# Layer 0's attention with seven PSUM banks in one ring of single places

## The chip, the cores and the metric

One Trainium2 chip; the kernel runs on one of its cores. The metric is the device time of one execution in microseconds (us), the median over several runs. All data are fp32. PSUM, the memory that the tensor engine (PE) writes its products to, has eight banks; one bank takes 128 partitions of 512 fp32 numbers. The other engines are named as in the profile: DVE (vector), ACT (scalar), POOL (GpSimd), SP (sync); PEld are PE's weight loads.

## The reference

Two transformer layers over x of 8 sequences, 512 tokens, width 256; each layer is attention and a mixture of experts, each followed by a residual sum and a layer norm. The change touches layer 0's attention (16 heads of 16 numbers, 8 sequences):

```python
qkv = x @ w_qkv + b_qkv
q, k, v = jnp.split(qkv, 3, axis=-1)          # to heads: [b, h, s, d]
scores = jnp.einsum('bhid,bhjd->bhij', q, k) * attn_scale
scores = jnp.where(j >= i, scores, -jnp.inf)  # i: row, j: column
attn = jax.nn.softmax(scores, axis=-1)
out = jnp.einsum('bhij,bhjd->bhid', attn, v)
out = out @ w_out + b_out                     # then x = layernorm(x + out)
```

A token attends to itself and to later ones. After this come layer 0's experts (seven with weights, two choices per token), layer 1's attention with sigmoid weights, and layer 1's experts.

## The kernel before

**Order.** Everything is issued in an order written out by hand (`tc.manual_schedule()`), so each engine works through its instructions as the Python code issues them. Each tile pool is a ring: the tile that is asked for as the n-th of a pool with `bufs` places lies where tile n - bufs lay, and its first writer waits until the last reader of that one is through.

**PSUM.** `psum(stack, sc, av, mm)` (L86) divides the eight banks into three pools: `sc`, wide places of two banks (`wide()`, L93); `av`, single banks for the sums of attention; `mm`, single banks for everything else (`bank()`, L96). Layer 0 runs with `psum(banks, 3, 1, 1)`: three wide places, one `av`, one `mm`. Layer 1 runs with (2, 2, 2).

**Layer 0's attention** is `waves0` (L1356). A sequence is 16 waves: two groups m of eight heads, two halves t of each with four heads (r = 0 to 3), and four blocks of 128 tokens. A wave g issues, in this order:
- `scores` (L624): four products of 32 rows of PE each, K block jb against the queries up to it, of 512, 384, 256 and 128 columns in the four waves of a group (written S512 to S128 below; L629). They go to two wide places, two heads in each. One exponential on ACT (L638) reads a wide place and writes both halves of a tile e; POOL zeroes the masked corner (`affine_select`, L641).
- on the third of four waves `lowered` (L614): PE turns a tile of row bounds (L619) into a single place, DVE copies it (L621), and a DMA puts it into the rows of q that shift the scores.
- first steps of `beside0` (L1286), the work of other sequences: projections of q and k (`query`, L571, read twice by ACT at L584), values (`value`, L556, read by ACT at L564 and L569), `projected` (L673, read by DVE at L683 and L684), transposes of x (`turned_in`, L539, read by ACT at L548), and small routing steps. Each product takes one single place.
- `greatest` (L595) for the wave six further on: four products again (L600; 128, 256, 384, 512 columns when S has 512, 384, 256, 128; written G below) into two wide places. DVE adds a mask and takes the bound of each row, one instruction a head (L608, `seen`), followed by a read of its accumulator, with which the place is free.
- `gathered` (L648): four products of the last wave's e with the values, into `av` (L653); at the end of a group ACT copies `av` out (L661).
- second steps of `beside0`.

In the places' terms a wave without further steps takes four wide places: S heads 0 and 1, S heads 2 and 3, G heads 0 and 1, G heads 2 and 3. The two places of a quad come from

```python
        def quad(width):
            pair = [wide(), wide()]
            return pair, [pair[r // 2][:, r % 2, :width] for r in range(NHS)]
```

Sequences 0 to 6 run first (112 waves), then layer 0's experts (`experts0`, L1412, PE with wide places, beside them the last steps of sequence 6), then the 16 waves of sequence 7 beside the first steps of layer 1, then layer 1. In sequence 0 and during sequence 3 some steps prepare the router's weights (`router_steps`, L307), one step a wave, through the single place.

Of the kernel before, what the change touches and what calls it, by code (L numbers as in the profile page):

```python
# [12 lines left out]
AF = mybir.ActivationFunctionType  # L13
ALU = mybir.AluOpType
AX = mybir.AxisListType
PSUM = bass.MemoryType.PSUM
# [7 lines left out]
NHS = 4  # L24
# [13 lines left out]
SCALE = 0.25  # L38
# [5 lines left out]
def tile_two_layers(  # L44
# [33 lines left out]
    nc = tc.nc  # L78
# [5 lines left out]
    p = {}  # L84

    def psum(stack, sc, av, mm):  # L86

        for name, bufs in (("sc", sc), ("av", av), ("mm", mm)):
            p[name] = stack.enter_context(
                tc.tile_pool(name=f"p_{name}{sc}", bufs=bufs, space=PSUM)  # L90
            )

    def wide():  # L93
        return p["sc"].tile([P, 2, 512], FP, tag="sc", name="sc")

    def bank():  # L96
        return p["mm"].tile([P, 512], FP, tag="mm", name="mm")
# [289 lines left out]
    moe0 = ExitStack()  # L387
    moew = moe0.enter_context(tc.tile_pool(name="moew", bufs=2, side="right"))
    banks = ExitStack()
    psum(banks, 3, 1, 1)  # L390
    nc.scalar.preload_act_table_set("natural_log_exp_and_others")

    def half(name):

        return att.tile([P, S], FP, tag="half", name=name, bufs=16)

    def pair(name):
        return att.tile([P, 2, S], FP, tag="e", name=name, bufs=5)

    def layer0():  # L400
# [13 lines left out]
        ps = bank()[:, : 2 * KC].rearrange("p (i m) -> p i m", m=KC)  # L414
# [153 lines left out]
                q["lg"] = small.tile([P, NC, 8], FP, tag="lgx0", name="lgx0", bufs=3)  # L568
            nc.scalar.copy(q["lg"][:, c, :], ps[:, D : D + 8])  # L569

        def query(b, m, which, part, place=bank):  # L571
            q = st[b]
            w, bias = (wq_s, bq_t) if which == "q" else (wk_s, bk_t)
            at = part * 256
            ps = place()
            for kc in range(KC):
                nc.tensor.matmul(
                    out=ps[:, :256], lhsT=w[:, kc, m * P : (m + 1) * P],
                    rhs=q["xT"][:, kc, at : at + 256], start=(kc == 0), stop=(kc == KC - 1),
                )  # L580
            for t in range(2):
                if part == 0:
                    q[which, m, t] = half(f"{which}{b}_{m}{t}")
                nc.scalar.activation(  # L584
                    q[which, m, t][:, at : at + 256], ps[:, :256], AF.Identity,
                    bias=bias[:, m, t : t + 1], scale=lanes[:, t : t + 1],
                )


        def quad(width):  # L590

            pair = [wide(), wide()]
            return pair, [pair[r // 2][:, r % 2, :width] for r in range(NHS)]

        def greatest(b, m, t, ib):  # L595
            q = st[b]
            width = S - ib * P
            _, places = quad(width)
            for r in range(NHS):
                nc.tensor.matmul(  # L600
                    out=places[r],
                    lhsT=q["q", m, t][32 * r : 32 * r + 32, ib * P : (ib + 1) * P],
                    rhs=q["k", m, t][32 * r : 32 * r + 32, ib * P :],
                    start=True, stop=True,
                )
            for r in range(NHS):
                seen = wp.tile([P, S], FP, tag="seen", name="seen")
                nc.vector.tensor_tensor_reduce(  # L608
                    out=seen[:, :width], in0=places[r], in1=shade[:, :width], scale=-1.0,
                    scalar=-MASKED, op0=ALU.add, op1=ALU.min,  # L610
                    accum_out=mpads[t][:, r, ib : ib + 1],
                )
# [11 lines left out]
        def scores(b, m, t, jb):  # L624
            q = st[b]
            width = (jb + 1) * P
            tiles, places = quad(width)
            for r in range(NHS):
                nc.tensor.matmul(  # L629
                    out=places[r],  # L630
                    lhsT=q["k", m, t][32 * r : 32 * r + 32, jb * P : (jb + 1) * P],
                    rhs=q["q", m, t][32 * r : 32 * r + 32, :width],
                    start=True, stop=True,
                )
            es = []
            for s in tiles:
                e = pair("e")
                nc.scalar.activation(e[:, :, :width], s[:, :, :width], AF.Exp, scale=SCALE)  # L638

                own = e[:, :, jb * P : width]  # L640
                nc.gpsimd.affine_select(  # L641
                    out=own, in_=own, pattern=[[0, 2], [-1, P]], compare_op=ALU.is_ge, fill=0.0,
                    base=0, channel_multiplier=1,
                )
                es += [e[:, u, :width] for u in range(2)]
            return b, m, t, jb, es
# [709 lines left out]
    def waves0(start, stop):  # L1356
        nonlocal waiting
        t = l0
        for g in range(start, stop):
            b, w = g // 16, g % 16  # L1360
            now = None
            if g >= 0:
                now = t.scores(b, w // 8, w // 4 % 2, NC - 1 - w % 4)
                if w in FILLS:
                    t.fill(b, FILLS.index(w))
                if w == 10 and b + 2 < B:
                    t.load_x(b + 2)
            if g % 4 == 3 and waiting:
                t.gathered(*waiting)
                waiting = None  # L1370
            if (g + 2) % 4 == 0 and 0 <= g + 2 < 16 * B:
                ob, ow = (g + 2) // 16, (g + 2) % 16
                t.lowered(ob, ow // 8, ow // 4 % 2)
            first, second = beside0(b, w if g >= 0 else g)
            if b == 0 and w in (1, 3, 4, 5, 8, 9, 12):
                fn, arg = t.rsteps.pop(0)
                fn(arg)
                if w == 1:
                    t.residual(0)
            if b in (1, 2):  # L1380
                for _ in range(2):
                    if loads:
                        nc.sync.dma_start(**loads.pop(0))
            if 16 * 3 + 10 <= g < 16 * 3 + 10 + len(l1.steps):
                fn, arg = l1.steps[g - 16 * 3 - 10]
                fn(arg)
            run(first)
            ob, ow = (g + AHEAD) // 16, (g + AHEAD) % 16
            if ob < B:
                t.greatest(ob, ow // 8, ow // 4 % 2, (1, 0, 3, 2)[ow % 4])  # L1390
            if waiting:
                t.gathered(*waiting)
            run(second)
            waiting = now
# [229 lines left out]
    l0 = layer0()  # L1624
    loaded = {}
    with tc.manual_schedule():
        for kc in range(KC):
            l0.turned_in(0, kc)
        for which in ("q", "k"):
            for part in range(2):  # L1630
                l0.query(0, 0, which, part, lambda: wide()[:, 0, :])
        waves0(-AHEAD, 16)
        l1 = layer1(Later(), SimpleNamespace(dma_start=lambda **copy: loads.append(copy)))
        waves0(16, 48)
        assert not loads
        for e in range(2):
            loaded[e] = weights0(e)
        waves0(48, 16 * (B - 2))
        h = [half(f"h{f}") for f in range(I0 // P)]
        waves0(16 * (B - 2), 16 * (B - 1) - 3)  # L1640

        xe = att.tile([P, 2, 2, S], FP, tag="o", name="xe", bufs=2)
        xes = {
            e: tokens0(e, xe[:, e].rearrange("p u (c d) -> p (u c) d", d=D)) for e in range(2)
        }
        waves0(16 * (B - 1) - 3, 16 * (B - 1))
        l0.gathered(*waiting)
        waiting = None
        a, z, n = B - 2, B - 3, B - 1
        t = l0  # L1650
        steps = [(t.apart_again, a)]
        steps += [(t.query, n, 1, "q", part) for part in range(2)]
        steps += [(t.inverted, a)]
        steps += [(t.query, n, 1, "k", part) for part in range(2)]
        steps += [(t.kept, z, c) for c in range(NC)]
        steps += [(t.shared, z), (t.pointed, z)]
        steps += [(t.weighed, a, kc) for kc in range(KC)]
        steps += [(t.counted, z), (t.filled,), (t.ranked, z), (t.sent, z)]
        steps += [(t.projected, a, c) for c in range(NC)]
        steps += [(fn, a) for fn in (t.rooted, t.normed, t.logits)]  # L1660
        steps += [(t.kept, a, c) for c in range(NC)]
        steps += [
            (fn, a) for fn in (t.chosen, t.raised, t.shared, t.pointed, t.counted, t.ranked, t.sent)
        ]
        experts0(loaded, xes, h, steps)
    moe0.close()
    planp = ctx.enter_context(tc.tile_pool(name="planp", bufs=1, side="right"))
    rows1 = ExitStack()
    l1p = rows1.enter_context(tc.tile_pool(name="l1p", bufs=1, side="right"))
# [13 lines left out]
    places = wide(), bank()  # L1683
# [164 lines left out]
    with tc.manual_schedule():  # L1848
# [3 lines left out]
        t, b = l1, B - 1  # L1852
# [248 lines left out]
```

## Time and profile before

| | us |
|---|---|
| median of 3 runs | 1477.97 (1472.56 to 1480.37) |
| the profiled execution's own time | 1483.55 |
| its span, first to last instruction | 1481.8 |
| layer 0's attention, sequences 0 to 6 | about 0 to 511 |
| layer 0's experts | about 511 to 721 |
| layer 0's attention, sequence 7 | about 721 to 785 |
| busy over the span: PE, PEld | 1374.9 (93%), 727.5 (49%) |
| busy over the span: DVE, ACT, POOL | 852.4 (58%), 692.1 (47%), 459.4 (31%) |
| DVE at L608 (512 reductions) | 251.0 |
| ACT at L638 (256 exponentials) | 168.2 |
| mean granted clock of PE | 0.966 |

The profile is of one execution; its engine rows are busy time, its groups give for each line the number of instructions, the busy time (overlaps counted once), the mean of one, and the engine's idle time before them with who ended it. A fp32 product shows as two records, so four heads are eight records. PE's quad of four heads runs side by side, each head on its own 32 rows. The table by windows gives busy time per stretch, the granted clock and the DMA engines' share. The waits name the waiting engine and line, and who ended the wait.

### The profile page before, as it was taken

The numbers are of one execution on the slowest core, as the hardware profiler recorded it, in microseconds if no ns is written. First come the engines' busy times: TensorE is split into PE (matmuls) and PEld (weight loads), VectorE is DVE, ScalarE is ACT, GpSimd is POOL, SyncE is SP. The second block draws the span as 40 slices with busy tenths as digits, with TensorE's granted clock in tenths as the row PEclk, the third lists the DMA queues.
The fourth block names the chain that finished last, engine by engine and source line by source line (L and its number), as shares of the span: only waits on it lengthen the run. The fifth ranks groups of instructions, "written<-read, shape, count | busy, mean of one in ns | idle before, by whom it ended". The sixth has DMA issues, their size and how long they took to land. (4 is left out here: it accounts for less than half of the span.)

```text
span 1481.8 us, 24146 instructions
## 1 busy us (share of the span) xinstructions
PE 1374.9 (93%) x8094; PEld 727.5 (49%) x8094; DVE 852.4 (58%) x3167; ACT 692.1 (47%) x1092; POOL 459.4 (31%) x580
## 2 busy tenths in 40 slices
PE   7999999899999899999989899999999999899991
PEld 4444444444443466766533333333333335788881
DVE  4556667666766523121367568777777754633494
ACT  3554655545554421111346657666766665122241
POOL 1322233334233200000263213544544232242562
PEclk9999999999998999999979889999999999999996
DMA  3555356333515232223242011232232026766864
GB/s 62 181 129 179 66 182 212 126 96 131 164 61 146 76 94 92 86 85 100 77 145 46 16 45 42 48 65 41 51 68 46 25 60 189 228 201 214 282 218 158
DMA packets 147483, 167.94 MB, mean 113 GB/s; under 512 B 36509, under 2 KB 126266, under 8 KB 147346
## 3 DMA queue, kind: packets, MB, share of 16 engines
q1 hardware_dynamic: 129746, 139.61, 31.7%
q0 software_dynamic: 10560, 23.51, 5.7%
q10 hardware_dynamic: 7040, 3.15, 0.8%
q8 instruction: 68, 1.11, 0.3%
q14 instruction: 69, 0.57, 0.1%
HBM read 85.27 MB, written 77.63 MB: 110 GB/s over the span
## 5 line engine op out<-in xcount | busy, mean ns | idle before, releaser
L608 DVE CUSTOM_DVE_ANT_0 seen<-sc,shade 128x128 f32<-128x128 f32 (+3 forms) x512 | 251.0, 490 | 155.1 <-PE sc L600 127.6
L1059 ACT ACTIVATE e<-sc 128x1024 f32<-128x1024 f32 x256 | 248.1, 1020 | 120.0 <-PE sc L1051 116.3
L641 POOL TENSOR_SCALAR_AFFINE_SELECT e<-e 128x256 f32<-128x256 f32 x256 | 104.1, 412 | 564.1 <-ACT e L638 559.6
L638 ACT ACTIVATE e<-sc 128x1024 f32<-128x1024 f32 (+3 forms) x256 | 168.2, 702 | 123.4 <-PE sc L629 116.1
L600 PE MATMUL sc<-k,q 32*128 32x384 f32 (+3 forms) x1024 | 143.4, 499 | 15.8 <-DVE mpad L608 7.3
L629 PE MATMUL sc<-q,k 32*128 32x512 f32 (+3 forms) x1024 | 137.3, 495 | 10.1 <-DVE mpad L608 8.5
L1068 PE MATMUL av<-e,v 128*32 128x512 f32 x1024 | 139.8, 619 | 0.0
L653 PE MATMUL av<-e,v 128*32 128x512 f32 (+3 forms) x1024 | 101.6, 466 | 1.5 <-POOL e L641 1.5
L600 PEld LDWEIGHTS sc<-k,q 32*128 32x128 f32 x1024 | 62.1, 190 | 75.7 <-DVE mpad L608 24.6
L1441 PE MATMUL sc<-xeT,wi 128*128 128x512 f32 x224 | 98.1, 593 | 0.4 <-DVE xeT L1427 0.4
L1458 PE MATMUL sc<-wo,h 128*128 128x256 f32 x448 | 98.3, 379 | 0.0
L1778 PE MATMUL yp<-w_e,h 128*128 128x256 f32 x416 | 95.0, 380 | 3.4 <-DVE h L1770 1.9
L1762 PE MATMUL sc<-xtT,w_e 128*128 128x256 f32 x416 | 97.5, 389 | 0.0
L629 PEld LDWEIGHTS sc<-q,k 32*128 32x128 f32 x1024 | 56.6, 190 | 68.9 <-issue 36.3
L1458 PEld LDWEIGHTS sc<-wo,h 128*128 128x128 f32 x448 | 84.7, 190 | 11.7 <-issue 0.5
L1051 PE MATMUL sc<-q,k 16*128 16x512 f32 x512 | 85.6, 663 | 3.6 <-PEq L1684 1.8
L1789 POOL DMA_INDIRECT ybuf<-yt,to x52 | 51.0, 982 | 117.7 <-DVE yt L1788 107.3
L1051 PE MATMUL sc<-q,kb 32*128 32x512 f32 x512 | 85.9, 640 | 1.5 <-ACT e L1059 1.4
L1778 PEld LDWEIGHTS yp<-w_e,h 128*128 128x128 f32 x416 | 78.5, 190 | 15.9 <-DVE h L1770 2.7
L1762 PEld LDWEIGHTS sc<-xtT,w_e 128*128 128x128 f32 x416 | 79.5, 196 | 11.0 <-issue 0.5
L1033 POOL TENSOR_TENSOR q<-raw,cos_s 128x512 f32<-128x512 f32 x16 | 20.6, 1289 | 191.0 <-ACT raw L1030 191.0
L1209 POOL DMA_INDIRECT xbuf<-x,idx x64 | 67.8, 1059 | 34.4 <-DVE kept L1203 19.3
(293 smaller groups left out, 1962.1 us busy)
## 6 DMA issues: line engine op xcount, KB each, us to landing
xbuf<-blank SPq DMA_DIRECT2D x130, 272.0 KB
w_e<-in_w SPq DMA_DIRECT2D x104, 256.0 KB
ybuf<-blank SPq DMA_DIRECT2D x16, 512.0 KB
ao<-o SPq DMA_DIRECT2D x128, 64.0 KB
aoT<-shares_d SPq DMA_DIRECT2D x16, 512.0 KB
y<-ybuf SPq DMA_DIRECT2D x16, 512.0 KB
wi<-in_we_in SPq DMA_DIRECT2D x7, 1024.0 KB
wo<-in_we_out SPq DMA_DIRECT2D x7, 1024.0 KB
```

Source lines behind the costliest of these rows:

```text
L600: nc.tensor.matmul(out=places[r], lhsT=q["q", m, t][32 * r : 32 * r + 32, ib * P : (ib + 1) * P], rhs=q["k", m, t][32 * r : 32 * r + 32, i ...
L608: nc.vector.tensor_tensor_reduce(out=seen[:, :width], in0=places[r], in1=shade[:, :width], scale=-1.0, scalar=-MASKED, op0=ALU.add, op1=AL ...
L629: nc.tensor.matmul(out=places[r], lhsT=q["k", m, t][32 * r : 32 * r + 32, jb * P : (jb + 1) * P], rhs=q["q", m, t][32 * r : 32 * r + 32, : ...
L638: nc.scalar.activation(e[:, :, :width], s[:, :, :width], AF.Exp, scale=SCALE)
L641: nc.gpsimd.affine_select(out=own, in_=own, pattern=[[0, 2], [-1, P]], compare_op=ALU.is_ge, fill=0.0, base=0, channel_multiplier=1,)
L653: nc.tensor.matmul(out=q["av"][32 * r : 32 * r + 32, : (jb + 1) * P], lhsT=vs[b % 2][:, jb, 8 * m + 2 * r + t, :], rhs=es[r], start=(jb == ...
L1051: nc.tensor.matmul(out=scs[r // 2][:, r % 2, :], lhsT=k[32 * r : 32 * r + lanes, jb * P : (jb + 1) * P], rhs=q["q", m][32 * r : 32 * r + l ...
L1059: nc.scalar.activation(e, scs[pr], AF.Sigmoid, scale=SCALE)
L1068: nc.tensor.matmul(out=q["av"][32 * r : 32 * r + 32, :], lhsT=vs[b % 2][:, jb, 8 * m + 2 * r + t, :], rhs=es[r // 2][:, r % 2, :], start=( ...
L1458: nc.tensor.matmul(out=ps[:, c, :], lhsT=h[f][:, c * P : (c + 1) * P], rhs=wo[:, f, :], start=(f == 0), stop=(f == I0 // P - 1),)
L1762: nc.tensor.matmul(out=ps[:, f // 2, f % 2 * TB : (f % 2 + 1) * TB], lhsT=q.wi[kc][:, f * P : (f + 1) * P], rhs=q.xtT[:, kc, :], start=(kc ...
L1778: nc.tensor.matmul(out=q.ps[c], lhsT=q.h[:, f // 2, at : at + P], rhs=q.wo[f // 2][:, f % 2 * D : (f % 2 + 1) * D], start=(f == 0), stop=( ...
```

## The change

Layer 0's attention takes all its products from one ring. `psum0` makes two pools, one bank for `av` and seven for `mm`. `quad` asks for four single places, one a head, from the ring that also serves the single products. The exponentials are issued one a head, two to a tile e; the `affine_select` still takes both halves of e at once. Around the experts of layer 0 the pools are closed and opened anew: (3, 1, 1) as before for the experts, `psum0` again for sequence 7. Layer 1 keeps (2, 2, 2).

```diff
+    def psum0(stack):
+        for name, bufs in (("av", 1), ("mm", 7)):
+            p[name] = stack.enter_context(
+                tc.tile_pool(name=f"p_{name}0", bufs=bufs, space=PSUM)
+            )
...
-    psum(banks, 3, 1, 1)
+    psum0(banks)
...
-        def query(b, m, which, part, place=bank):
+        def query(b, m, which, part):
...
-            ps = place()
+            ps = bank()
...
-            pair = [wide(), wide()]
-            return pair, [pair[r // 2][:, r % 2, :width] for r in range(NHS)]
+            return [bank()[:, :width] for r in range(NHS)]
...
-            _, places = quad(width)
+            places = quad(width)
...
-            tiles, places = quad(width)
+            places = quad(width)
...
-            for s in tiles:
+            for pr in range(2):
                 e = pair("e")
-                nc.scalar.activation(e[:, :, :width], s[:, :, :width], AF.Exp, scale=SCALE)
+                for u in range(2):
+                    nc.scalar.activation(
+                        e[:, u, :width], places[2 * pr + u], AF.Exp, scale=SCALE
+                    )
...
         waves0(16 * (B - 1) - 3, 16 * (B - 1))
         l0.gathered(*waiting)
         waiting = None
+        banks.close()
+        psum(banks, 3, 1, 1)
...
         experts0(loaded, xes, h, steps)
     moe0.close()
+    banks.close()
+    psum0(banks)
```

The four first projections of sequence 0, which took a wide place each, also take single places.

More of the change, by code (lines that the diff above doesn't have):

```diff
@@ L1630, in tile_two_layers @@
             for part in range(2):
-                l0.query(0, 0, which, part, lambda: wide()[:, 0, :])
+                l0.query(0, 0, which, part)
         waves0(-AHEAD, 16)
```

## The prediction

> **What bounds the kernel now.** I read the page's slices first (PE at nine tenths nearly throughout), then the table by windows for the two stretches that hold layer 0's attention; columns are busy us of PE, PEld, DVE, ACT, POOL, then clock and DMA.
>
> ```profile
> 40.00:505.00 465.00, 430.36 (x3198) 203.62 (x3196) 301.55 (x1296) 239.55 (x453) 150.91 (x273) 0.98 0.46 138
> 719.00:804.00 85.00, 76.24 (x506) 32.10 (x508) 51.25 (x174) 47.24 (x75) 42.35 (x62) 0.88 0.37 113
> ```
>
> PE is the bound: idle 34.6 + 8.8 = 43.4 us of 550. DVE (65%) and ACT (52%) have room on the mean. So the change can win only PE's idle time, and time that PE looks busy while a quad of products is cut in two. Who ends PE's idle time (waits of PE, 40 to 505 us: total, times, longest):
>
> ```profile
> PE sc L600 <- ACT e L638: 6.0, 12, 0.5
> PE sc L600 <- DVE mpad L608: 5.7, 13, 0.5
> PE sc L629 <- DVE mpad L608: 5.3, 10, 1.2
> PE mm L619 <- ACT k L584: 3.3, 7, 0.5
> PE mm L577 <- ACT q L584: 2.2, 2, 1.1
> ```
>
> All five are waits for a PSUM place to be read: three for a wide place, two for the one single place. The groups by shape (80 to 560 us) show the cut quads:
>
> ```profile
> L629 PE MATMUL sc<-q,k 32*128 32x512 f32 x200 | 44.0, 635 | 4.0 <-DVE mpad L608 3.3 <-issue 0.7
> L600 PE MATMUL sc<-k,q 32*128 32x512 f32 x208 | 36.1, 687 | 0.3 <-DVE mpad L608 0.3
> L638 ACT ACTIVATE e<-sc 128x1024 f32<-128x1024 f32 x50 | 49.3, 1022 | 20.7 <-PE sc L629 20.0
> L638 ACT ACTIVATE e<-sc 128x768 f32<-128x768 f32 x50 | 37.8, 806 | 12.0 <-PE sc L629 12.0
> L638 ACT ACTIVATE e<-sc 128x512 f32<-128x512 f32 x50 | 27.1, 596 | 34.4 <-PE sc L629 33.7
> L638 ACT ACTIVATE e<-sc 128x256 f32<-128x256 f32 x50 | 17.0, 384 | 23.0 <-PE sc L629 22.9
> ```
>
> A quad of S (L629) at 512 columns holds PE 44.0/25 = 1.76 us, the same quad of G (L600) 36.1/26 = 1.39. The timeline of one hand-over in wave 7 to 8 shows why:
>
> ```profile
> 401.22 0.69 DVE L608 CUSTOM_DVE_ANT_0 seen<-sc,shade 128x512 f32<-128x512 f32 x1 [1.42 <-PE sc L600]
> 401.26 0.70 PE L629 MATMUL sc<-q,k 32*128 32x512 f32 x2
> 401.96 0.69 DVE L608 CUSTOM_DVE_ANT_0 seen<-sc,shade 128x512 f32<-128x512 f32 x1
> 402.50 1.02 ACT L638 ACTIVATE e<-sc 128x1024 f32<-128x1024 f32 x1 [0.80 <-PE sc L629]
> 402.71 1.13 PE L629 MATMUL sc<-q,k 32*128 32x512 f32 x4 [0.32 <-DVE mpad L608]
> 402.80 0.69 DVE L608 CUSTOM_DVE_ANT_0 seen<-sc,shade 128x512 f32<-128x512 f32 x1
> 403.53 0.69 DVE L608 CUSTOM_DVE_ANT_0 seen<-sc,shade 128x512 f32<-128x512 f32 x1
> ```
>
> S's first two heads start at 401.26, the others at 402.71, when DVE has reduced G's second head (end 402.65). Note the steps of DVE: 0.74 within a wide place, 0.84 across two, 0.73 again.
>
> **The change, part by part.** *Ring.* Before, a wide place waits for the one three back. After, a head waits for the tile seven back, and the single places stand in the same ring. A sequence takes 128 + 23 tiles in 16 waves, 9.4 a wave: 7/9.4 = 0.74 wave of lookahead, against 6/8 = 0.75. So the ring is hardly longer; it is finer, and the separate wait for the single place goes.
>
> *Exponentials.* The four rows fit 0.172 us + 0.828 ns per element. 256 more instructions are 44 us of ACT by durations, but two in a row overlap:
>
> ```profile
> 364.03 1.08 ACT L638 ACTIVATE e<-sc 128x512 f32<-128x512 f32 x2
> ```
>
> 2 x 0.596 = 1.19, so 0.11 overlaps and each added one costs about 0.07: 17 us of ACT, beside PE. [...] What matters is when a place comes free: the first head's exponential ends 0.39 us (768 elements) to 0.43 us (1,024) before the pair's did, the second's 0.07 after it.
>
> *Reductions.* Each head's reduction now waits for its own product. The row steps above price that: 0.11 us where a new PE wait stands beside the wait for DVE's own last result. Before, one step of three paid; now all do: 0.22 a quad, 128 quads, 28 us of DVE, beside PE until DVE is late. [...]
>
> *Where it decides.* I walked one steady sequence (the 65.9 us from G512 at 385.1 us) by hand, quad by quad: a quad goes when PE is through and its last place is read, with the lengths of the timeline kept (S and G 0.43, 0.64, 0.85, 1.07 us for 128 to 512 columns; av 0.36 to 1.0; single tiles about 1.1; read latencies as in the timeline). The locks:
> - S512 after G512: with no single tile between them (wave 7) the last head waits for G's first head instead of its second: 401.98 instead of 402.71, 0.73 won. With one between them (waves 3, 11, 15) it still waits for the second, 0.11 later: nothing won.
> - G256 after S384: the last pair waited for S's first pair, 1.02 + 0.81 = 1.83 us after S's start; now for the first head, 1.51: 0.3 won, with S384's own earlier places up to 0.8, in waves 1 and 5. In 9 and 13 a single tile between hides it or moves it to the second head.
> - G384 after S256 (every fourth wave, always bound): last head on the second head's exponential: 0.07 lost.
> - G128 after G512's fourth head: 0.22 lost where PE arrives early.
> - Single places: the 10 us or so of waits before L619, L577 and L677 go, but L619 stands before the bound G384 and the L577 of waves 3 and 11 before the bound S512, so half of that returns as a longer next wait.
> - Waves 8, 9 and 12, 13: DVE also reads projected's tiles, and ACT's exponentials stand behind rooted, which waits for DVE: of 1.1 us won by wave 8, 0.3 goes by wave 9; of 0.8 at wave 12, 0.4 is left at wave 14.
>
> PE's lead over before, in us: 0.8 (wave 5), 1.1 (8), 0.8 (9), 0.8 (12), 0.4 (14), 0.75 (15), 1.0 (wave 2 of the next sequence). DVE and ACT lead by as much there, so it repeats: 1.0 us a sequence.
>
> *Once.* Router steps of sequence 0 and of L337's chain, which queue for the one single place: 1.5 won (rows of 1.2 and 0.8 at L337). Sequence 7, half of it without G: 1.0 won. Three hand-overs of the banks: the first wide place of the experts and of layer 1 now covers av's old bank and waits for its copy (0.59 + 0.1), the first scores of sequence 7 for the last expert's two copies (0.69 + 0.59): between 0 and 4, I take 2.5 lost.
>
> Sum: -7 x 1.0 - 1.5 - 1.0 + 2.5 = -7.0 us. Affine selects hide what ACT delays: their results lie 1.2 us or more before the product that needs them.
>
> The profiled execution took 1483.55 us (span 1481.8): 1476.5 after. It lies 5.6 us above the median 1477.97; on the median the forecast is **1471**.
>
> **The rivals.**
> - *Larger gain.* If the walk's returns at DVE are too harsh, the first-order count holds: the waits of each quad against the ring's new releases, on before's own times, fall by about 38 us in all; half of that kept is -20: 1458. The clock may add: it is halved in places of this stage, as here,
>
> ```profile
> 454.00:468.00 14.00, 14.00 (x81) 5.93 (x77) 8.46 (x39) 4.92 (x9) 2.81 (x7) 0.52 0.76 245
> ```
>
> where waves 4 to 7 took 15.3 us (453.30 to 468.57) against 11.9 in the sequence before, which had a 1.1 us tile more: 4.5 us lost. It follows gaps (PE idle 0.68 and 0.45 us before 451.72 and 453.30). Some 41 us of this stage ran so, 13 us lost; shorter gaps could save part, another rhythm could lose as much. Chance 0.16.
> - *Nothing.* DVE's 0.22 a quad takes the rest: PE's lead closes in waves 8 to 14 wholly. For: DVE would be busy 10.7 + 0.9 = 11.6 of 16.2 us per four waves, and it works in bursts. 0 to -3 us, 1475 to 1478. Chance 0.19.
> - *Slower: halves of one tile take turns.* The two exponentials of a pair write halves of one e. If the second waits for the first's end, the overlap becomes a gap, as with the experts' two halves:
>
> ```profile
> 512.51 0.69 DVE L1427 COPY xeT<-sc 128x512 f32<-128x512 f32 x1
> 513.23 0.59 ACT L1428 COPY xeT<-sc 128x512 f32<-128x512 f32 x1 [1.52 <-DVE xeT L1427]
> ```
>
> Here ACT starts its half 0.03 after DVE ends the other. Against: those are two engines; four writes of 0.41 us into parts of one xn by one engine take 1.52 together (timeline at 759.94). Priced: step +0.17 to +0.27 a head: G384 +0.2 four times, S384 +0.5 three times a sequence, 2.2 lost against 1.0 won, 8 times: +10, 1488. It decides from about 0.12 us more a step. [...] Chance 0.23, with lost clock.
> - *It does not do what it says* (the ring still waits in pairs): as "nothing".
>
> **How the numbers follow.** Forecast (-2 to -14) 0.42. What a measurement can tell from no change is 0.5%, 7.4 us. Faster by more: 0.24 of the forecast and the 0.16: 0.40. Within: 0.18 and 0.19: 0.37. Slower: 0.23. The likeliest case alone spans 1464 to 1476; the range takes in the larger gain with some clock (1452) and the slower case (1489).
>
> **What would show it.** Right: S512 of wave 8 whole (1.1 us, not 1.76); no PE wait at L619 or L577 for ACT; DVE's steps of G512 all 0.84; exponentials of a pair overlapping by 0.1; S512 to S512 of the same wave 64.9 us apart instead of 65.9; DVE's busy time unchanged but its gaps shorter. Wrong: exponentials with a gap between them, G384 or S384 waiting longer than before, a first quad after a change of banks idle for over 2 us, or another number of half-clock stretches moving the time more than all this.

## The result and the profile after

The kernel after takes **1465.4 us** (median of 19 runs, 1458.13 to 1474.67) against 1481.19 for the kernel before in the same comparison (19 runs): ratio **0.9888, 95% interval 0.9869 to 0.9908**, 16.6 us faster. The forecast was 7 us. The profiled execution took 1465.97 us (span 1464.3; before 1483.55 and 1481.8).

The code moved by a few lines: products S are at L635 (were L629), G at L606 (L600), exponentials at L645 (L638), reductions at L614 (L608), lowered at L625 (L619), query and key at L584 (L577). First the windows of the same two stretches of the kernel after; columns as before: PE, PEld, DVE, ACT, POOL, clock, DMA.

```profile
36.00:488.00 452.00, 442.03 (x3218) 225.57 (x3216) 301.82 (x1301) 251.58 (x678) 151.90 (x274) 0.98 0.47 142
702.00:788.00 86.00, 79.40 (x496) 33.68 (x494) 50.35 (x172) 48.31 (x105) 41.71 (x61) 0.82 0.37 112
```

PE's idle time in the first stretch fell from 34.6 to 452.00 - 442.03 = 10.0 us, but its busy time rose from 430.4 to 442.0: a quad that waits for its places one head at a time looks busy while it waits. DVE does the same work in less time, ACT has its added instructions and is still at 56%. The second stretch (sequence 7) won nothing; the clock there was 0.82 instead of 0.88. PE's waits in 36 to 488 us of the kernel after, all that are listed:

```profile
PE mm L606 <- DVE mpad L614: 5.2, 15, 0.4
PE mm L625 <- DVE mpad L614: 2.3, 6, 0.5
PE mm L344 <- DVE turns L341: 1.7, 2, 0.9
```

No wait for ACT is left, neither at a wide place nor at the single one (L619 and L577 of before). What remains is DVE. The groups by shape, 80 to 540 us of the kernel after:

```profile
L645 ACT ACTIVATE e<-mm 128x512 f32<-128x512 f32 x100 | 51.6, 602 | 12.3 <-PE mm L635 11.7
L635 PE MATMUL mm<-q,k 32*128 32x512 f32 x200 | 45.9, 633 | 0.0
L606 PE MATMUL mm<-k,q 32*128 32x512 f32 x200 | 32.5, 640 | 0.0
```

The idle time in front of L635 is gone and a quad of G512 (L606) takes 32.5/25 = 1.30 us instead of 1.39, yet a quad of S512 holds PE 45.9/25 = 1.84 us, not less than the 1.76 of before. The timeline of the hand-over of wave 7 to 8 in the kernel after (DVE, PE and PEld rows of reductions and S, and the exponentials) shows it:

```profile
387.65 1.03 PE L635 MATMUL mm<-q,k 32*128 32x512 f32 x3
387.81 0.69 DVE L614 CUSTOM_DVE_ANT_0 seen<-mm,shade 128x512 f32<-128x512 f32 x1 [0.69 <-PE mm L606]
...
388.56 0.29 PEld L635 LDWEIGHTS mm<-q,k 32*128 32x128 f32 x2 [0.28 <-DVE mpad L614]
388.65 0.69 DVE L614 CUSTOM_DVE_ANT_0 seen<-mm,shade 128x512 f32<-128x512 f32 x1
388.87 2.06 ACT L645 ACTIVATE e<-mm 128x512 f32<-128x512 f32 x4 [0.45 <-PE mm L635]
389.49 0.69 DVE L614 CUSTOM_DVE_ANT_0 seen<-mm,shade 128x512 f32<-128x512 f32 x1
...
389.61 1.16 PE L686 MATMUL mm<-wo_s,aoT 128*128 128x264 f32 x4
390.33 0.69 DVE L614 CUSTOM_DVE_ANT_0 seen<-mm,shade 128x512 f32<-128x512 f32 x1
```

Only the fourth head waits, 0.28 us for G's first reduction, and the next product starts 1.96 us after the quad did. Before, that was 2.51 us: the quad started at 401.26 and the next product at 403.77.

```profile
403.77 1.16 PE L677 MATMUL mm<-wo_s,aoT 128*128 128x264 f32 x4
```

DVE's steps are all 0.84 in the kernel after. Four exponentials of 0.602 take 2.06: (4 x 0.602 - 2.06)/3 = 0.12 us overlap each, so they do not take turns.

### The profile page after: what moved, and what is told of

Its sections match the earlier page's. It is cut to its first block, busy times and chain, and to the rows that moved or that the text cites. A ratio compares the mean times of both kernels' runs of the same rounds, so it can differ in the third digit from the quotient of the medians.

```text
span 1464.3 us, 24915 instructions
## 1 busy us (share of the span) xinstructions
PE 1385.6 (95%) x8094; PEld 750.4 (51%) x8094; DVE 850.6 (58%) x3167; ACT 705.0 (48%) x1348; POOL 459.0 (31%) x580
## 5 line engine op out<-in xcount | busy, mean ns | idle before, releaser
L614 DVE CUSTOM_DVE_ANT_0 seen<-mm,shade 128x128 f32<-128x128 f32 (+3 forms) x512 | 250.5, 489 | 153.8 <-PE mm L606 93.1
L645 ACT ACTIVATE e<-mm 128x256 f32<-128x256 f32 (+3 forms) x512 | 182.4, 443 | 107.0 <-PE mm L635 98.2
L606 PE MATMUL mm<-k,q 32*128 32x384 f32 (+3 forms) x1024 | 164.2, 501 | 8.7 <-DVE mpad L614 7.0
L635 PE MATMUL mm<-q,k 32*128 32x512 f32 (+3 forms) x1024 | 140.3, 497 | 1.5 <-ACT ye L1474 1.5
L606 PEld LDWEIGHTS mm<-k,q 32*128 32x128 f32 x1024 | 84.3, 192 | 59.8 <-DVE mpad L614 23.2
L635 PEld LDWEIGHTS mm<-q,k 32*128 32x128 f32 x1024 | 60.3, 192 | 62.2 <-issue 36.9
```

The lines of the kernel that those rows point to most:

```text
L606: nc.tensor.matmul(out=places[r], lhsT=q["q", m, t][32 * r : 32 * r + 32, ib * P : (ib + 1) * P], rhs=q["k", m, t][32 * r : 32 * r + 32, i ...
L614: nc.vector.tensor_tensor_reduce(out=seen[:, :width], in0=places[r], in1=shade[:, :width], scale=-1.0, scalar=-MASKED, op0=ALU.add, op1=AL ...
L635: nc.tensor.matmul(out=places[r], lhsT=q["k", m, t][32 * r : 32 * r + 32, jb * P : (jb + 1) * P], rhs=q["q", m, t][32 * r : 32 * r + 32, : ...
L645: nc.scalar.activation(e[:, u, :width], places[2 * pr + u], AF.Exp, scale=SCALE)
```

## Where the time came from

First S512 of each sequence in both traces, and PE's lead of the kernel after over before:

| | before, us | after, us | lead, us |
|---|---|---|---|
| sequence 0 | 34.7 | 30.6 | 4.1 |
| sequence 1 | 99.8 | 97.8 | 2.0 |
| sequence 2 | 164.8 | 161.0 | 3.8 |
| sequence 3 | 231.0 | 225.8 | 5.2 |
| sequence 4 | 305.0 | 293.7 | 11.3 |
| sequence 5 | 370.9 | 358.7 | 12.2 |
| sequence 6 | 436.8 | 423.5 | 13.3 |
| layer 0's experts | 510.9 | 491.7 | 19.2 |
| sequence 7 | 721.2 | 704.4 | 16.8 |
| layer 1, first scores | 783.5 | 768.3 | 15.2 |
| end | 1481.8 | 1464.3 | 17.5 |

Sequences 1, 2, 4 and 5, all at full clock, win 1.8, 1.4, 0.9 and 1.1 us, 1.3 on the mean; the forecast was 1.0. Sequence 0 loses: after had 10.2 us of half clock in it (the order-of-banks kernel below, with none there, took 63.4 us for it, before 65.1). Three places hold what the forecast did not have: the stretch ahead of sequence 0, sequence 3 (74.0 to 67.9 us) and sequence 6 (to the experts, 74.1 to 68.2). In each the kernel before waits for the one single place. PE's waits of the kernel before ahead of 36 us, without the one for DMA that both have:

```profile
PE mm L619 <- ACT q L584: 1.1, 1, 1.1
PE mm L560 <- ACT q L584: 1.1, 1, 1.1
PE mm L545 <- ACT xT L548: 0.7, 1, 0.7
```

2.9 us, and none of it for ACT is left after. The rest of the 4.1 is clock: before had 3.4 us of half clock ahead of sequence 0 and after had none. The order-of-banks kernel, which is after with 3.4 us of half clock there, starts at 32.0 instead of 30.6, so 1.4 us of the 4.1 go with the clock and 2.7 are left. In sequence 6 (436 to 511 us) of before

```profile
PE sc L629 <- DVE mpad L608: 2.5, 3, 1.2
PE mm L577 <- ACT q L584: 2.2, 2, 1.1
```

the L577 row is waves 8 and 9, where a query and a key product stand one behind the other; their waves fall from 7.9 and 7.2 us to 6.2 and 6.0. In sequence 3, waves 11, 14 and 15 (router steps) fall from 5.4, 4.8 and 8.1 to 4.4, 3.6 and 5.8 us; 3.4 us of half clock in wave 15 of before are 1.7 of that. Sequence 6 had 17.1 us of half clock before and 10.2 after, so some 3 us of its 5.9 may be clock too. The pair with three buffers (below) has full clock in all three places: there sharing wins 2.8 us ahead of sequence 0 (31.8 to 29.0), 6.2 in sequence 3 (70.6 to 64.4) and 5.2 in sequence 6 (65.7 to 60.5).

**How far the clock enters.** Over 39 runs of the kernel before, time and mean granted clock go together: a line through them gives 12 us for each 0.01 (correlation -0.89). The clock of after was 0.9637 on the mean against 0.9656, so by this line the clock took some 2 us from the change. The table below gives this share for every kernel; as the line is that of one kernel, the shares of the others are estimates.

## The experiments

Theory A at the outset: the gain beyond the forecast is the single products', which got more than one place. Rival: the finer places and the one-head exponentials bring it. "Against before" is ratio and interval, "us" the same times 1481 us; "clock" is the share by the line above; "sequence 5" is S512 to S512 in the profile, at full clock, but for the last row.

| kernel | against before | us | clock | sequence 5, us |
|---|---|---|---|---|
| before | 1 | 0 | 0 | 65.9 |
| after | 0.9888 [0.9869, 0.9908] | -17 | +2 | 64.8 |
| one-head exponentials alone | 0.9997 [0.9959, 1.0034] | 0 | -4 | 66.8 |
| split places | 1.0177 [1.0131, 1.0222] | +26 | +6 | 67.0 |
| split places, fair start | 1.0153 [1.0107, 1.0198] | +23 | +10 | 67.0 |
| after, reductions in turned order | 0.9781 [0.9734, 0.9828] | -32 | -8 | 63.7 |
| before, three buffers | 0.9837 [0.9806, 0.9868] | -24 | -9 | 64.9 |
| split, three buffers | 0.9896 [0.9848, 0.9943] | -15 | -3 | 64.9 |
| after, three buffers | 0.9674 [0.9640, 0.9708] | -48 | -10 | 62.5 |
| after, order of banks | 0.9877 [0.9841, 0.9913] | -18 | -2 | 64.8 |
| after, three buffers and order | 0.9654 [0.9626, 0.9683] | -51 | -12 | 62.5 |
| split, five and two | 1.0349 [1.0285, 1.0413] | +52 | +19 | 76.9 |

**Split places** (after, but no sharing):

```
-        for name, bufs in (("av", 1), ("mm", 7)):
+        for name, bufs in (("qd", 6), ("av", 1), ("mm", 1)):
...
-            return [bank()[:, :width] for r in range(NHS)]
+            return [
+                p["qd"].tile([P, 512], FP, tag="qd", name="qd")[:, :width] for r in range(NHS)
+            ]
```

> The kernel after, but the seven places are no longer shared: the quads of products take turns on six single banks of their own, and the single products (query, key, value, lowered, projected, xT, router) have one bank for themselves, as before. One-head places and one-head exponentials stay. Theory A (what was won beyond the forecast came from the single products having more than one place: prologue, router steps, the sequences in which they stand between quads): the waits of PE for ACT at the query and xT lines return, the first quad of S starts near 34.5 us again instead of 30.6, waves 10 to 15 of sequence 3 lose their 4 us, and the time lies within 5 us of the kernel before (ratio 0.997 to 1.003). Rival B (the finer places of the quads and the one-head exponentials alone bring it): the prologue still loses its 4 us but the rest is kept, 10 to 13 us faster than before (0.991 to 0.993).

It was slower than before, outside both. 10 us of that is the start (first S512 at 45.1 us, before 34.7): before had the first query and key in wide places, this version in the one single bank. The rest is new: without sharing, the finer places cost.

**Split places, fair start** mends the first part; the first four query and key products take the quads' banks:

```
-                l0.query(0, 0, which, part)
+                l0.query(
+                    0, 0, which, part,
+                    lambda: p["qd"].tile([P, 512], FP, tag="qd", name="qd"),
+                )
```

> The split places once more (six single banks for the quads, one bank for the single products), but the four products of the first query and key take the quads' banks, as they do in the kernel before (in the first split version they had only the one bank, and the first quad came at 45.1 us instead of 34.7). What is left against before is only that a quad's places and exponentials are of one head each, so this is the change without its sharing. Theory A (finer places bring about 0, and the extra 0.11 us of every second reduction costs 1.3 us a sequence): 8 to 14 us slower than before (1.005 to 1.010), so the sharing alone is worth 25 to 30 us. Rival B (finer places bring the walk's 1.0 us a sequence): 5 to 8 us faster (0.995 to 0.997).

The sign is theory A's: +23 us, S512 to S512 67.0. The mean clock was 0.957, by the line some 10 of the 23, and the 13 that are left lie in theory A's range. So the sharing is worth 2.2 us a sequence (67.0 to 64.8), and the rest of the change costs 1.1 (65.9 to 67.0). The waves of the one single place stay: waves 8 and 9 of sequence 6 take 8.1 and 7.2 us, wave 11 of sequence 3 takes 5.4. PE's waits in its sequence 6 (442 to 518 us) show the row of before again, with the new line numbers:

```profile
PE mm L584 <- ACT q L591: 2.2, 2, 1.1
```

**One-head exponentials alone** (before, wide places kept):

```
-                nc.scalar.activation(e[:, :, :width], s[:, :, :width], AF.Exp, scale=SCALE)
+                for u in range(2):
+                    nc.scalar.activation(e[:, u, :width], s[:, u, :width], AF.Exp, scale=SCALE)
```

> The kernel before with one edit: the exponential of two heads is cut into two exponentials of one head, the wide places stay. A place of two heads is now read 0.07 us later (the second exponential's end). Theory A: only that lock costs, at G384 after S256 and G256 after S384 together about 0.3 to 0.5 us a sequence: 1 to 4 us slower than before (1.001 to 1.003). Rival B (the two halves of one tile take turns, the slower case of the prediction): gaps in place of overlaps, 10 us slower (1.007). Rival C (the earlier first exponential lets the selects and the products after them go sooner, a gain of its own): 3 us or more faster (below 0.998).

No difference in the total that this interval can show; it excludes 10 us. But by the line 4 us of gain went with a higher clock, and the four sequences that ran at full clock in both profiles (1, 2, 4 and 5) took 0.4, 0.2, 0.7 and 0.9 us more than in before. That is theory A's small loss rather than nothing. "Halves of one tile take turns" falls, and so does a gain from earlier selects.

**What the rest costs: the reductions' second wait.** In these traces a reduction that waits for PE and for an earlier DVE result has the second wait as an instruction of its own in front of it. These rows count them for the 512 reductions of before, of after, and of after with three buffers; all but one or two in each row wait for a DVE result:

```profile
L608 DVEq EVENT_SEMAPHORE  x205: 21/21/21, 17.8 to 762.3; - x103
L614 DVEq EVENT_SEMAPHORE  x446: 21/21/21, 15.5 to 749.1; - x149
L614 DVEq EVENT_SEMAPHORE  x256: 21/21/21, 16.2 to 714.9; - x128
```

In before and after none of them starts while a reduction is running. Two experiments make these waits fewer or let them be met earlier. The first turns the order, so that the second of each two finds its product done:

```
-            for r in range(NHS):
+            for r in (1, 0, 3, 2):
```

> The kernel after with the four reductions of a quad in the order head 1, 0, 3, 2, so that the wait for PE of the second of each two is met already and every other step should fall from 0.84 to 0.73 us (0.61 to 0.71 at 384 columns), as in the kernel before. DVE saves 2 x 0.11 us a quad, 28 us in all. Theory A (this is the term that the prediction sized at a small return): 6 to 10 us faster than the kernel after, 1455 to 1460 (0.982 to 0.986 of before). Rival B (a place is freed later, since head 0's is read second: 0.73 us later for the first, as much sooner for the second): no gain or a loss of up to 6 us.

180 such waits are left, the steps of G512 are 0.73, 0.84, 0.73, as in before, and sequences take 1.1 us less than after's. In all it is 16 us faster than after, more than theory A said; about 10 of that goes with the granted clock (0.9726 on the mean against 0.9637), 5 to 7 us are left, against 1.1 us times eight sequences = 8.8. The second gives the throw-away result three buffers instead of two, so that a reduction waits for an older result. 256 of the separate waits are still there (third row above), but 235 of them start while a reduction is still running:

```
-                seen = wp.tile([P, S], FP, tag="seen", name="seen")
+                seen = wp.tile([P, S], FP, tag="seen", name="seen", bufs=3)
```

> The kernel after with three instead of two buffers for the throw-away result of the head's reduction, so that fewer reductions have to wait for an earlier reduction beside their wait for PE. Theory A (the reductions' step of 0.84 us holds the quads back, as the prediction had it): the steps of G512 fall to 0.74 or below where the second wait is gone, DVE saves some 10 to 20 us of waiting and the time falls by 2 to 5 us against the kernel after (0.986 to 0.987 of before). Rival B (the step is the price of the wait for PE alone, whatever stands beside it): steps stay 0.84, time within 1 us of the kernel after. Rival C (steps fall, but DVE is not what PE waits for): steps fall, time within 1 us.

Theory A in kind, but the steps fell to 0.61, below the 0.74 that I had as the floor, and the time by 32 us, not 2 to 5; by the line some 12 of the 32 are clock. DVE's timeline of this kernel:

```profile
387.01 0.69 DVE L614 CUSTOM_DVE_ANT_0 seen<-mm,shade 128x512 f32<-128x512 f32 x1 [3.61 <-PE mm L606]
387.63 0.08 DVE L614 DVE_READ_ACCUMULATOR2_ANT mpad<- 128x1 f32 x1
387.63 0.69 DVE L614 CUSTOM_DVE_ANT_0 seen<-mm,shade 128x512 f32<-128x512 f32 x1
388.24 0.08 DVE L614 DVE_READ_ACCUMULATOR2_ANT mpad<- 128x1 f32 x1
388.24 0.69 DVE L614 CUSTOM_DVE_ANT_0 seen<-mm,shade 128x512 f32<-128x512 f32 x1
...
388.85 0.69 DVE L614 CUSTOM_DVE_ANT_0 seen<-mm,shade 128x512 f32<-128x512 f32 x1
```

A reduction now starts while the accumulator of the last is being read, 0.07 to 0.08 us before that reduction's end. DVE is through with a G512 2.53 us after its start (388.85 + 0.69 - 387.01) and not at 3.21, and PE is hardly idle: its window, 34 to 460 us, has 426.00 - 423.73 = 2.3 us idle at full clock.

```profile
34.00:460.00 426.00, 423.73 (x3208) 224.11 (x3207) 276.09 (x1300) 248.25 (x675) 150.61 (x274) 1.00 0.51 151
```

The same edit on before and on the split places:

> The kernel before with one edit: three instead of two buffers for the throw-away result of the head's reduction (the same edit took 32 us off the kernel after). Theory A (a reduction that waits both for PE and for an earlier reduction costs 0.11 us more, one that waits for an earlier reduction 0.12 us more than one that does not; before pays the first once in three steps, after in each): the steps of 0.73 and 0.84 us fall to 0.61, the time falls by 15 to 25 us to 1457 to 1467 (0.983 to 0.990), so less than after gained, because the single place and the wide places still hold PE. Rival B (reductions matter only since the change made every one of them wait twice): below 8 us (above 0.995). Rival C (DVE's steps are all there is, the ring nothing): as fast as after with the same edit, 1434 (0.967).

> The split places (six single banks for the quads, one for the single products, first query and key in the quads' banks) with three buffers for the reductions' throw-away result, so that the price of the reductions' second wait is gone here too. Against the kernel before with the same three buffers (1456, ratio 0.984) it differs only in the grain of the quads' places and exponentials. Theory A (all that the split kernel lost against before came from DVE's second waits, and finer places bring nothing or little): 1450 to 1458 (0.981 to 0.986), sequences of 64 to 65 us. Rival B (finer places do bring 1.0 us a sequence once DVE is quick): 1445 to 1449 (0.977 to 0.980). Rival C (finer places cost by themselves, through exponentials or locks): above 1460 (0.988).

On before it won 24 us (some 9 of it clock), theory A. The split kernel with three buffers has the 64.9 us of before with three buffers in sequence 5, so finer places bring nothing by themselves and, with the waits met early, cost nothing there. Its median (1464 us) lies in rival C's range, and its interval reaches into theory A's; of its 9 us behind before with three buffers some 6 go with the clock, and the rest is not traced. The two parts nearly add in a steady sequence: three buffers win 1.0 on before, 2.1 on split, 2.3 on after; sharing wins 2.2 with two buffers and 2.4 with three.

**Five and two** (the fair split kernel with other numbers):

```
-        for name, bufs in (("qd", 6), ("av", 1), ("mm", 1)):
+        for name, bufs in (("qd", 5), ("av", 1), ("mm", 2)):
```

> As the split kernel with the first query and key in the quads' banks, but five single banks for the quads and two for the single products. Theory A (what the prediction sized too small is the single products' wait for their one place: it shows in the prologue, in sequence 3 with the router steps, which took 74.0 us before and 67.9 after, and at the end of sequence 6): sequence 3 is only 3 to 4 us longer than sequence 2, instead of 8, as in the kernel after; the other sequences are longer than the split kernel's 67.0 by 1 to 3 us since a quad's ring is shorter; in all 1490 to 1505 (1.005 to 1.015). Rival B (the quads' lookahead is what the sharing gives): sequence 3 still 7 us longer than sequence 2, in all over 1510 (1.02).

The total, 52 us slower, is in rival B's range (over 1510), but the half clock lies so unevenly in sequences 2 and 3 (30.7 and 3.4 us) that their lengths, which were to decide, cannot be compared. On the waves theory A: with a second single place, and nothing shared, wave 9 of sequence 6 falls from 7.2 to 5.9 and wave 11 of sequence 3 from 5.4 to 4.4, wave 14 takes 3.6: the values of the kernel after (6.0, 4.4, 3.6). That settles those terms; wave 8 of sequence 6 had half clock and tells nothing. Five places for quads cost about 5 us in a sequence at full clock, not 1 to 3 (70.9 and 72.1 in sequences 1 and 4 against 65.9 and 67.3), and the clock, by the line, took some 19 us:

```profile
72.00:300.00 228.00, 226.87 (x1361) 111.81 (x1361) 125.66 (x532) 110.30 (x291) 53.23 (x106) 0.89 0.47 137
300.00:560.00 260.00, 257.52 (x1591) 128.87 (x1594) 155.63 (x682) 126.34 (x335) 85.83 (x148) 0.92 0.34 103
```

PE is idle 3.6 us in these 488.

**Order of banks**, the hand-over term:

```
-        for name, bufs in (("av", 1), ("mm", 7)):
+        for name, bufs in (("mm", 7), ("av", 1)):
```

> The kernel after with the order of its two groups of banks exchanged in layer 0 (the seven places first, the bank of av last), so that the first wide place of the experts and of layer 1 lies on banks of the ring and not on av's. Theory A (the hand-overs cost the 2.5 us that the sum has for them, and the wait for av's copy is half of it): 1 to 2 us faster than the kernel after, seen as shorter gaps of PE at the first product of the experts and of layer 1. Rival B (what a new place waits for ends just as late whichever bank it is, because the last tiles of the ring are the ones in use): within 0.7 us of the kernel after, the gaps as long, only released by another line.

Rival B. At the experts' first product PE's wait in the kernel after is

```profile
PE sc L1432 <- issue: 1.9, 1, 1.9
```

and in this one

```profile
PE sc L1432 <- DVE mpad L614: 2.0, 1, 2.0
```

just as long. In the kernel after, av's copy ended at 490.54 us, and the product started at 491.66, just behind DVE's last accumulator read (491.48 to 491.56): the last reductions set the wait, not av's bank. At layer 1's first scores it falls from 0.9 to 0.5. The remaining change of banks, ahead of sequence 7, has a wait in the kernel after too, at the first scores for the last expert's copy:

```profile
PE mm L635 <- ACT ye L1474: 1.5, 1, 1.5
```

In before PE does not wait at the first product of any of the three, but 0.4 us each shortly behind the experts' and sequence 7's. The intervals of after and of this kernel overlap almost wholly.

**Three buffers and order**, the version to keep:

> The kernel after with three buffers for the reductions' throw-away result and the order of the two groups of banks exchanged, as the version to keep. If the two edits add: 1429 to 1433 (0.965 to 0.968 of before), 0 to 3 us faster than with the three buffers alone. If the hand-over is hidden in the faster kernel: the same as with three buffers alone, 1434.

Median 1426.92 us, 51 us under before and faster than before and after; against three buffers alone (1433.58) the intervals overlap, so the second edit is not shown to help.

## Why the prediction was right, and where its sum was short

The direction, the range (1452 to 1489) and the gain of a steady sequence held. The size of the sum did not: the 16.6 us lie between the forecast's 2 to 14 and the larger gain's 20. Where a number below came out for another reason than the one given, that is luck.

- **The steady sequences** (7 x 1.0): right in size. 1.8, 1.4, 0.9 and 1.1 were measured where no router step and no stretch of half clock lies in between; S512 to S512 of the same wave in sequence 5 is 64.8 (forecast 64.9). But the reason given for it, "the ring is hardly longer; it is finer", had it the wrong way about. The split kernels are the finer ring without the seventh place, and they win nothing. Sharing is worth 2.2, and the reductions' waits return 1.1. The locks that the walk counted (fourth head after G's first) are those of seven shared places; how much of the 2.2 is theirs, and how much is the single products' shorter waits in these sequences, is not separated.
- **Reductions, 0.22 a quad**: the size of the step was right (0.84 throughout, 241 more separate waits of 0.11 = 27 us of DVE against 28 forecast). What PE loses by it is a sequence's 1.1 us, and the clock's share came on top in the turned order: with 180 of these waits instead of 446 a sequence takes 1.1 us less (63.7 against 64.8). Not seen in the prediction: the wait that cost most was there in both kernels, the one for DVE's own result, 0.12 us of each step within a wide place too (0.734 against 0.612 with three buffers).
- **Once, 1.5**: this term was far too small. It took the router steps' rows alone and let the rest of the single place's waits return "as a longer next wait". Ahead of sequence 0 some 2.7 us were won at equal clock, in waves 11 and 14 of sequence 3 1.0 + 1.2, in waves 8 and 9 of sequence 6 1.7 + 1.2: together 7.8. The row "PE mm L577 <- ACT q L584: 2.2, 2, 1.1" stood in the prediction; its two waves won 2.9, so nothing of it returned.
- **Sequence 7, 1.0**: open. It took 62.3 us to layer 1 before and 63.8 after, but with 30.7 us of half clock after against 20.5; its first wave, at full clock in both, fell from 3.4 to 2.3.
- **Hand-overs, 2.5 lost**: too small. The waits are 1.85 + 1.46 + 0.88 = 4.2, against 0.8 in before: 3.4 lost, within its "between 0 and 4". The wait ahead of sequence 7 had its reason and about its size (1.5 for 1.3). The reason for the first (av's old bank) is not shown: another order of banks left it as it was. In the table of leads the experts' stretch lost 2.4, but after had 3.4 us of half clock in it and before none.
- **The sum again**: -7 x 1.3 for the sequences, -7.8 once, -1.0 left for sequence 7 and +3.4 for the hand-overs give -14.5, against -16.6. The rest is not traced.
- **S512 of wave 8 whole**: in part. 0.55 won instead of 0.73, since the fourth head still waited 0.28 us for G's first reduction. The sign that was named, 1.1 us for a quad of S512 instead of 1.76, did not come: the group shows 1.84, because a quad that waits head by head counts as busy.
- **Exponentials**: the first head's was to end 0.39 us sooner at 768 elements; by the prediction's own fit it is 0.806 - 0.490 = 0.32. The lock that uses it (1.83 to 1.51) has the right difference, so the sum is not touched.
- **The rivals.** Larger gain: its size nearly came, not its reason, for the clock did not bring it, and the excess lay at single products, which its count of the quads' waits does not hold. Nothing: DVE did take back, but a half. Slower, halves take turns: excluded; the exponentials overlap by 0.12, and the one-head exponentials alone cost 0.2 to 0.9 us a sequence where 2.2 was priced.
- **"It follows gaps"**, of the half clock: not borne out by idle time as the profile shows it. The five-and-two kernel has PE idle 3.6 of 488 us and ran at 0.89 and 0.92; before idled 34.6 of 465 at 0.98. A quad in single places looks busy while it waits, so the gaps that are left inside it are not known.

## What to carry to other kernels

A single buffer through which producers of different kinds queue is priced wave by wave: where the next product was waiting anyway I had its wait come back, an estimate that no run here singles out; where two such products stood one behind the other it did not (2.9 us won in waves 8 and 9 of sequence 6), and the few places of this kind brought 7.8 us beside the 9.1 of seven steady sequences. Before making places finer, look at what each reader must wait for besides: a scratch output that nobody reads still made nearly every reduction wait for the one before it (446 of 512 in the kernel after, by the row above), and a third buffer for it won about as much as the change itself (on the kernel before 24 us against 17; by the line of the clock, at equal clock 15 against 19). And split a gain into its parts with the clock beside it: the granted clock differed by 0.01 between these kernels (0.9637 on the mean in after, 0.9733 in before with three buffers), and in the runs of the kernel before 0.01 went with 12 us.

## What the runs showed of the hardware that I had not expected

- By the trace's semaphore records, the step of DVE's reductions of 512 columns with two buffers (on before) is 0.734 us where they wait for an earlier DVE result alone, 0.843 where they wait for PE as well; with three buffers (on before) 0.612 with a wait for a DVE result, 0.611 with one for PE and 0.617 with none, and in the timeline of after with three buffers 0.62, 0.61 and 0.61. So a wait that is met while the reduction before is still running costs nothing here, and the wait for the result just before costs this pair of reduction and accumulator read 0.12 us (0.734 against 0.612).
- In the clock records of before and after the half clock comes in multiples of 3.4 us (3.4, 6.8, 10.2, 13.7, 20.5 and 27.3), but for the stretch that the end of each run cuts off (29.2 and 28.4). Busy time as the profile gives it does not tell which kernel will lose the clock: after with three buffers had PE busy 423.73 of 426 us at 1.00, five and two 226.87 of 228 at 0.89. Why after with three buffers kept it full through sequences 0 to 6, and five and two lost it, stays open.
